# A four-layer image network on one core: in the scans, lines of one pair of images alone at the turns, small products in their pauses, an early pool for the scans' weights, and layer 3's loads in written order

## The chip, the cores and the metric

The kernel runs on one core of one Trainium2 chip. The metric is the device time of one execution in microseconds (us). Three runs of the kernel before gave a median of 13183.47 us (13182.98 to 13188.03).

The core has five engines that matter here, each with an instruction order of its own: TensorE (PE, matrix products), VectorE (DVE), ScalarE (ACT), GpSimd (POOL) and SyncE (SP, which only starts transfers). ACT and POOL can start transfers too. A profile row "L678 PE" is what line 678 of the kernel gave to PE.

## The reference, cut to what matters

The input is four images of 48 channels, 256 by 256, in fp32. Four layers each add something to the image. Layers 1 and 2 are the scans that the change is mostly about:

```python
def step(w, b):
    def f(carry, inp):
        nxt = inp + _conv1d(carry, w, b)     # 5 taps, 48 -> 48 channels, along the line
        return (nxt, nxt)
    return f
...
_, d_rest = jax.lax.scan(step(down_w, down_b), d0, xs[1:])    # rows, from above
...
_, u_rest = jax.lax.scan(step(down_w, down_b), u0, seq)       # rows, from below
...
_, r_rest = jax.lax.scan(step(right_w, right_b), r0, ws[1:])  # columns
...
_, l_rest = jax.lax.scan(step(left_w, left_b), l0, R[Ww - 2::-1])
...
x = x + _L0_conv_ref(_gn(x), ...)   # 1x1, depthwise 3x3, gate, 1x1, filter on 8x8 patches
x = x + _L1_conv_ref(_gn(x), ...)   # the four scans
x = x + _L2_conv_ref(_gn(x), ...)   # the four scans, other weights
x = x + _L3_conv_ref(_gn(x), ...)   # 1x1, filter on 8x8 patches, depthwise 3x3, gate, 1x1
```

`_gn` is a group normalization over the whole image, so each layer needs the statistics of all of its input. In a scan each line of the image (a row or a column) needs the line before it: 256 lines in each of four directions, two layers, and no line of one image can be computed beside another of the same image.

## The kernel before

**Stages.** `input_stats` loads the input and takes its statistics. `layer0` runs with an order that a planner has written out for PE, DVE and ACT. `scans` does layers 1 and 2, `layer3` the last one. They follow one another; the scans run from about 3021 to 8550 us.

**The scans.** The four images are two pairs, A (p=0) and B (p=1). A line of a pair holds 96 partitions: the two interleaved halves of the line times 48 channels, and 256 columns for the two images. One line is three fp32 products into one PSUM tile (`conv`, L678; the profile records each as two rows, six rows a line) and one DVE instruction that adds bias and input and writes the line (the evict): L766 in the down pass, L804 up, L843 right, L881 left. The next line of the same pair reads that line, so a pair alternates between PE and DVE. Two pairs are therefore interleaved: while DVE evicts A's line, PE has B's.

**The order of the two.** `pair(p)` is a Python generator which yields after each line and between the pieces of a normalization (`norm_steps`). `scans` calls the two in turn, one step each a round, and B begins when `count` is 10. The order in which the instructions are written in this loop is the order on PE and on DVE (both are under `manual_schedule`), and it is fixed: if A's instruction waits, B's behind it on the same engine waits too. The other engines' instructions are placed by the scheduler. 36 small products (`WARM`, L704) stand in front of the first line.

**The turns.** Each pass of `scan_layer` goes in blocks of eight lines (`RB`). Down loads the input (L741 and, for the first block, 16 small loads at L750, on SP), scales it on ACT (L757, L761) and stores its lines to `dn`. Up reads `dn` (from its second block on), and ACT copies its lines to `blk` (L811), which goes to `up` (L816). Right reads `up` transposed (L831, on SP). Its first lines need the last rows of the up pass, through the copy, the store and the load; L840 copies its first line from that load. Left takes the lines of right from SBUF and then from `rt`, adds them onto a block of the input (L891; on POOL, and on DVE for the last block of the pass) and stores the sum (L897). It also takes the statistics of the new image (`bn_stats`, made as small functions in `fresh` and written at L904). Then `norm_steps` turns these into scale and shift: L109 aggregates, then two small products (L112, L120) with DVE and ACT pieces between them (L114 to L132).

**Weights.** `scan_weights` makes one direction's weight tile from ten small transfers and two for the bias (L648, L651). Layer 1's down weights are loaded when the scans open (on ACT's queue); right and left follow after A's first down pass, on SP's. Layer 2's are loaded between B's passes. A queue takes its transfers in order: what an issue waits for, all later ones on that engine wait for.

**Layer 0's and layer 3's start.** Both load weights on SP: layer 0 at L191 to L215, then scale and shift (`scp`, L240) and the raw image (L250); ACT normalizes it (L259), and the first product is at L289. Layer 3 fetches a raw strip (L956), copies the scale (`scp`, L945), loads `wi` (L965) and `mk_in` (L966), an identity (L979), depthwise and output weights (L984 to L1005), normalizes on ACT (L1024) and transposes on PE (L1039). Of the engines it fixes PE, DVE and ACT; SP is left to the scheduler.

Of the kernel before, what the change touches and what calls it, by code (L numbers as in the profile page):

```python
# [17 lines left out]
C = 48  # L18
# [11 lines left out]
WARM = 36  # L30


class Net:
# [63 lines left out]
    def norm_steps(self, stats, grp, name="", psum=None):  # L97

        nc, n, rows = self.nc, len(stats), stats[0].shape[0]
        with ExitStack() as st:  # L100
# [7 lines left out]
            for p in range(n):  # L108
                nc.vector.bn_aggr(mv[:, p, :], stats[p])  # L109
                yield  # L110
            pm = psum("pm")
            nc.tensor.matmul(pm, grp, mv[:, :, 0], start=True, stop=True)  # L112
            yield
# [4 lines left out]
            yield  # L118
            pv = psum("pv")
            nc.tensor.matmul(pv, grp, col(2), start=True, stop=True)  # L120
            yield
            nc.vector.tensor_scalar(col(3), pv, EPS, None, ALU.add)  # L122
            nc.scalar.activation(col(4), col(3), AF.Sqrt)  # L123
            yield
# [511 lines left out]
    def scan_weights(self, n, which, eng=None):  # L636


        nc, eng = self.nc, eng or self.nc.sync
        w = self.wp1.tile([CC, 3, CC], F32, name=f"w{n}_{which}", tag=f"w_{which}")  # L640
        b = self.wp1.tile([CC, 1], F32, name=f"b{n}_{which}", tag=f"b_{which}")
        nc.gpsimd.memset(w, 0.0)
        taps = self.a[f"L{n}_{which}_w"]
        for e in range(2):
            for f in range(2):
                lo, hi = (1 if e < f else 0), (2 if e > f else 3)
                for t in range(lo, hi):
                    eng.dma_start(  # L648
                        w[e * C : (e + 1) * C, t, f * C : (f + 1) * C], taps[:, 2 * t + e - f, :]
                    )  # L650
            eng.dma_start(b[e * C : (e + 1) * C, :], self.a[f"L{n}_{which}_b"])  # L651
        self.scan_w[n, which] = w, b

    def open_scans(self, st):
# [6 lines left out]
        self.lines, self.turn, self.scan_w = [], [0] * self.NP, {}  # L661
        self.scan_weights(1, "down", self.nc.scalar)
# [18 lines left out]
    def scans(self, first, stats):  # L681
# [18 lines left out]
        with self.tc.manual_schedule(engines={mybir.EngineType.PE, mybir.EngineType.DVE}):  # L700
            with self.tc.tile_pool(name="ps_w", bufs=1, space=PSUM) as psw:
                warm = psw.tile([128, 128], F32, name="warm")
                for _ in range(WARM):
                    self.nc.tensor.matmul(warm, self.ident, self.ident, start=True, stop=True)  # L704
            going, count = [pair(p) for p in range(self.NP)], 0
            while going:
                for p, g in enumerate(list(going)):
                    if count >= (2 * RB - 6) * p and next(g, g) is g:
                        going.remove(g)
                count += 1  # L710
        return last

    def scan_layer(self, n, p, x, xout, scs, stats):
# [20 lines left out]
        for h0 in range(0, H, RB):  # L734
# [3 lines left out]
            for f in range(2):  # L738
# [8 lines left out]
                for lo, hi in ((1, WB), (0, 1)):  # L747
                    for i in range(2):
                        for e in range(2):
                            nc.sync.dma_start(  # L750
                                half(t, f)[:, i, e, lo:hi].rearrange("p v h w -> p v (h w)"),
                                rows[:, i, e, lo:hi].rearrange("c v h w -> c v (h w)"),
                            )
            for i in range(2):
# [24 lines left out]
        if n == 1 and p == 0:  # L779
            self.scan_weights(1, "right")  # L780
            self.scan_weights(1, "left")
# [41 lines left out]
        for w0 in range(0, W, RB):  # L823
# [3 lines left out]
            for lo, hi in ((1, HB), (0, 1)) if w0 < 2 * RB else ((0, HB),):  # L827
                for e in range(2):
                    for i in ((0, 1), (1, 2)) if w0 < 2 * RB else ((0, 2),):
# [6 lines left out]
                        )  # L836
            for r in range(RB):
# [20 lines left out]
        for w0 in range(W - RB, -1, -RB):  # L858
# [29 lines left out]
            for lo, hi in ((0, RB), (RB, M)) if w0 == 0 else ((0, M),):  # L888
                for f in range(2):
# [3 lines left out]
                    )  # L893
                for e in range(2) if k == 0 else ():
# [10 lines left out]
        for f in fresh:  # L905
            f()

    def layer3(self, x, scs):  # L910
# [11 lines left out]
        with ExitStack() as st:  # L922
# [4 lines left out]
            st.enter_context(tc.manual_schedule(engines=FIXED))  # L927
# [35 lines left out]
            for lo, at, n in parts:  # L963
                for b in range(2):
                    nc.sync.dma_start(wi[64 * b : 64 * b + C, at : at + n], self.a["L3_w_in"][:, lo : lo + n])  # L965
                nc.sync.dma_start(mk_in[:, at : at + n], self.a["L3_fft_mask"][:, lo : lo + n])  # L966
# [448 lines left out]
def net_kernel(ctx: ExitStack, tc: tile.TileContext, args, out, shape):  # L1415
# [4 lines left out]
    first = net.layer0(scs, stats)  # L1420
    with ExitStack() as st:
        net.open_scans(st)
# [100 lines left out]
```

## Time and profile before

| what | value |
|---|---|
| median of three runs | 13183.47 us |
| profiled execution | 13184.79 us |
| span of that execution, first to last instruction | 13182.9 us |
| PE busy | 12347.8 us (94%) |
| DVE busy | 7413.1 us (56%) |
| ACT busy | 3603.9 us (27%) |
| mean granted clock of TensorE | 0.969 |
| first product of layer 0 | at 245.6 us |
| first conv of the scans | at 3040.4 us |
| last evict of the scans | at 8549.7 us |
| layer 3's first normalization (L1024) | at 8580.8 us |

Times of instructions are us from the start of the span. A row of the groups or of the timeline gives the duration, engine, line, output and inputs; in brackets is how long the engine was idle before the instruction and what ended that idle time. A row of the stretches gives for each engine its busy time and, in brackets, its instructions, then the clock that TensorE was granted as a fraction of full speed, then how busy the DMA engines were and what they moved. Busy time of PE is modelled from pipelined products.

### The profile page before, as it was taken

What the parts mean: (1) busy time and instruction counts of PE and PEld (TensorE: products, weight loads), DVE (VectorE), ACT (ScalarE), POOL (GpSimd) and SP (SyncE); (2) the same over time, 40 slices, a digit from 0 to 9 for tenths busy, and PEclk for the clock granted to TensorE, in tenths of its full rate; (3) what the DMA queues carried; (4) which work ended last, traced back from release to release, by engine and by line L of the source; (5) the groups of instructions that cost most, each with busy time, mean ns of one, the idle gap of its engine ahead of it and who ended that gap; (6) DMA issues with size and microseconds to landing.
All of it is one profiled execution on the core that took longest, in us unless ns stands there. A gap on an engine that the chain in (4) does not pass through costs nothing.

```text
span 13182.9 us, 432539 instructions
## 1 busy us (share of the span) xinstructions
PE 12347.8 (94%) x203416; PEld 8136.5 (62%) x203416; DVE 7413.1 (56%) x10790; ACT 3603.9 (27%) x4047; POOL 1333.8 (10%) x977
## 2 busy tenths in 40 slices
PE   2999999999999899999998999899999999999999
PEld 1333333336777677767776777666666666666666
DVE  6777777773333334653333346566666666666666
ACT  1444444442223100012232000033333333333333
POOL 0111010100000002530000015400000000000000
PEclk9999999998999999999999999899999999999999
DMA  7222222226755876987657769711111111111110
GB/s 174 57 57 58 57 55 58 59 48 114 152 141 152 168 153 152 229 174 152 135 151 169 153 134 225 183 25 28 28 23 28 24 26 28 23 27 23 27 28 21
DMA packets 1170373, 1225.00 MB, mean 93 GB/s; under 512 B 1027668, under 2 KB 1031756, under 8 KB 1107724
## 3 DMA queue, kind: packets, MB, share of 16 engines
q1 hardware_dynamic: 1067660, 624.28, 25.0%
q0 software_dynamic: 87488, 445.55, 11.8%
q10 hardware_dynamic: 13440, 127.50, 5.2%
q8 instruction: 1592, 26.08, 0.9%
q14 instruction: 193, 1.58, 0.0%
HBM read 699.76 MB, written 497.42 MB: 91 GB/s over the span
## 4 chain that ended last, share of the span: by engine, by line
PE 88%; ACT 4%; DVE 3%; issue 3%; DMA 2%; SPq 0%; ACTq 0%; POOL 0%; DVEq 0%
PE acc L678 41%; PE pd L1156 13%; PE pd L312 9%; PE pd L1172 5%; PE pz L1073 4%; PE pp L1120 4%; PE po L1248 2%; PE ph L289 2%; PE pz L1086 2%; PE ph L281 1%; PE py L386 1%; DMA gx<-in_x 1%; PE po L456 1%; PE py L393 1%; PE po L1238 1%
## 5 line engine op out<-in xcount | busy, mean ns | idle before, releaser
L678 PE MATMUL acc<-line,w_down 96*96 96x256 f32 x12240 | 2693.4, 382 | 36.3 <-DVE line L766 17.8
L678 PEld LDWEIGHTS acc<-line,w_down 96*96 96x96 f32 x12240 | 2007.8, 164 | 713.4 <-DVE line L766 32.5
L1156 PE MATMUL pd<-z_a,diag 32*32 32x512 f32 x37152 | 1628.5, 598 | 78.9 <-issue 71.2
L312 PE MATMUL pd<-main,diag 32*32 32x512 f32 x36864 | 1419.3, 619 | 55.0 <-issue 52.1
L678 PE MATMUL acc<-line,w_right 96*96 96x256 f32 x6120 | 1338.1, 379 | 82.0 <-issue 39.8
L678 PE MATMUL acc<-line,w_left 96*96 96x256 f32 x6120 | 1360.6, 384 | 27.3 <-DVE line L881 27.3
L1216 DVE SCALAR_TENSOR_TENSOR acc<-z_b,wd,acc 128x1024 f32<-128x1024 f32 (+1 forms) x1056 | 1325.8, 1258 | 34.2 <-ACT acc L1211 6.9
L349 DVE SCALAR_TENSOR_TENSOR acc<-rest,wd,acc 128x1024 f32<-128x1024 f32 x1024 | 1256.4, 1284 | 127.9 <-ACT acc L343 104.8
L1156 PEld LDWEIGHTS pd<-z_a,diag 32*32 32x32 f32 x37152 | 879.1, 103 | 636.9 <-issue 270.9
L678 PEld LDWEIGHTS acc<-line,w_right 96*96 96x96 f32 x6120 | 998.8, 163 | 411.5 <-DVE line L840 40.7
L678 PEld LDWEIGHTS acc<-line,w_left 96*96 96x96 f32 x6120 | 1007.0, 165 | 371.6 <-DVE line L881 41.5
L312 PEld LDWEIGHTS pd<-main,diag 32*32 32x32 f32 x36864 | 502.8, 105 | 767.1 <-issue 650.5
L1172 PE MATMUL pd<-z_b,diag 32*32 32x512 f32 x18432 | 966.6, 636 | 0.7 <-ACT z_b L1032 0.7
L766 DVE TENSOR_TENSOR line<-acc,in 96x256 f32<-96x256 f32 x1020 | 429.1, 421 | 949.5 <-PE acc L678 939.4
L843 DVE SCALAR_TENSOR_TENSOR line<-acc,b_right,in 96x256 f32<-96x256 f32 x1020 | 489.4, 480 | 835.5 <-PE acc L678 835.5
L804 DVE SCALAR_TENSOR_TENSOR line<-acc,b_down,in 96x256 f32<-96x256 f32 x992 | 476.0, 480 | 810.5 <-PE acc L678 810.5
L881 DVE SCALAR_TENSOR_TENSOR line<-acc,b_left,in 96x256 f32<-96x256 f32 x992 | 475.9, 480 | 557.4 <-PE acc L678 557.3
L123 ACT ACTIVATE nrm<-nrm 96x2 f32<-96x2 f32 (+1 forms) x7 | 1.4, 203 | 2823.4 <-DVE nrm L122 2783.6
L891 POOL TENSOR_TENSOR blk<-blk,line 96x1024 f32<-96x1024 f32 x248 | 705.8, 2876 | 638.0 <-DVE line L881 638.0
L811 ACT COPY blk<-line 96x1024 f32<-96x1024 f32 (+2 forms) x264 | 480.1, 1891 | 989.9 <-DVE line L804 803.9
L1076 DVE TENSOR_TENSOR z<-pz,mask 128x1024 f32<-128x1024 f32 x512 | 599.3, 1218 | 265.5 <-PE pz L1073 262.6
L1120 PEld LDWEIGHTS pp<-c_inv,z 64*64 64x64 f32 x32768 | 515.5, 135 | 225.3 <-issue 199.6
(169 smaller groups left out, 13063.5 us busy)
## 6 DMA issues: line engine op xcount, KB each, us to landing
blk<-x ACTq DMA_DIRECT2D x64, 1536.0 KB, 17.8
in<-x SPq DMA_DIRECT2D x248, 384.0 KB, 11.0
dn<-line POOLq DMA_DIRECT2D x124, 768.0 KB, 9.4
rt<-line POOLq DMA_DIRECT2D x124, 768.0 KB, 9.7
in<-rt SPq DMA_DIRECT2D x124, 768.0 KB, 10.8
in<-dn SPq DMA_DIRECT2D x120, 768.0 KB, 5.3
in<-up SPq DMA_DIRECT2D x240, 384.0 KB, 10.8
up<-blk POOLq DMA_DIRECT2D x56, 1536.0 KB, 15.1
```

Of the source, the lines that this page charges most:

```text
L312: nc.tensor.matmul(pd[32 * j : 32 * j + 32, i], diag[s, t, :], z[s, R2 * j + t // 3 : R2 * j + t // 3 + R2, t % 3 : t % 3 + W], start=(t = ...
L349: nc.vector.scalar_tensor_tensor(to, at(t, r), wd[:, 1, t : t + 1], to, ALU.mult, ALU.add)
L678: self.nc.tensor.matmul(acc, w[:, t, :], carry[:, :, t : t + m], start=(t == 0), stop=(t == 2))
L811: nc.scalar.copy(blk[:, :, e, lo:hi, k // 2 : k // 2 + RH], inner(ln[:, e::2])[..., lo:hi].rearrange("p h i w -> p i w h"),)
L843: nc.vector.scalar_tensor_tensor(blocks(inner(line)), blocks(acc), br, new, ALU.add, ALU.add)
L891: (nc.vector if w0 == 0 else nc.gpsimd).tensor_tensor(part, part, inner(ln[:, f::2])[..., lo:hi].rearrange("p w i h -> p i h w"), ALU.add)
L1073: nc.tensor.matmul(pz[:, b, q, :], xf[s, q0 + q, :], wi[s, NM * k : NM * k + NM], start=True, stop=True)
L1076: nc.vector.tensor_tensor(zs[k][:, q0 : q0 + 4].rearrange("p q b c -> p b q c"), pz, mask[:, :, :, NM * k : NM * k + NM].to_broadcast([128 ...
L1120: nc.tensor.matmul(pp[64 * c : 64 * c + 64, l, q, :], z[f, q0 + q, b, 64 * c : 64 * c + 64], self.inv1[f, :], start=True, stop=True,)
L1156: nc.tensor.matmul(pd[32 * j : 32 * j + 32, i, 0:n, :], diag[s, 2 if g == "m" else half, t, :], zt[g][s, R2 * j + t // 3 : R2 * j + t // 3 ...
L1172: nc.tensor.matmul(pd[to, i], diag[s, half, t, :], zt[f"b{half}"][s, R2 * j + t // 3 : R2 * j + t // 3 + R2, t % 3 : t % 3 + W], start=(t ...
L1216: nc.vector.scalar_tensor_tensor(acc, at(t), wd[:, half, t : t + 1], acc, ALU.mult, ALU.add)
```

## The change

There are four parts.

First, the scans' order. `pair` may yield a number instead of nothing. When it does and both pairs are active, two small products are written, and then the other pair does that many steps alone, each followed by two small products. The numbers are 2 before layer 2's first activations, 10 before a first right line, and 0 (two products, no lines) after each DVE piece of a normalization, each of the four additions of the last left block and each two of the last four statistics. When only one pair is active, each round ends with two small products. B begins at 11 rounds instead of 10. A yield of any kind takes a step of its own, and the other pair goes on with a line in it; so at a turn the other pair does 12 lines in a row, at a layer's end some 16. The small products write a PSUM tile that stays open through the scans; those in front are 60 instead of 36.

Second, the scans' weights live in a pool of their own which is opened before layer 0, and all three tiles of layer 1 are loaded there, on SP's queue, before layer 0's weights (36 transfers).

Third, half of the first block's loads of A in layer 1 go on ACT's queue.

Fourth, in layer 3 SP's order is as written, and the twelve loads of `wi` and `mk_in` go on ACT's queue.

```diff
-WARM = 36
+WARM = 60
+LEAD = 16
...
             for p in range(n):
                 nc.vector.bn_aggr(mv[:, p, :], stats[p])
-                yield
+                yield 0
...
-        w = self.wp1.tile([CC, 3, CC], F32, name=f"w{n}_{which}", tag=f"w_{which}")
-        b = self.wp1.tile([CC, 1], F32, name=f"b{n}_{which}", tag=f"b_{which}")
+        w = self.sw.tile([CC, 3, CC], F32, name=f"w{n}_{which}", tag=f"w_{which}")
+        b = self.sw.tile([CC, 1], F32, name=f"b{n}_{which}", tag=f"b_{which}")
...
-        self.lines, self.turn, self.scan_w = [], [0] * self.NP, {}
-        self.scan_weights(1, "down", self.nc.scalar)
+        self.warm = pool("ps1_w", 1, space=PSUM).tile([128, 128], F32, name="warm")
+        self.lines, self.turn = [], [0] * self.NP
...
-            going, count = [pair(p) for p in range(self.NP)], 0
+            def warm(k):
+                for _ in range(k):
+                    self.nc.tensor.matmul(self.warm, self.ident, self.ident, start=True, stop=True)
+
+            going, count = {p: pair(p) for p in range(self.NP)}, 0
+
+            def line(p):
+
+                got = next(going[p], going)
+                if got is going:
+                    del going[p]
+                return got
+
+            warm(WARM)
             while going:
-                for p, g in enumerate(list(going)):
-                    if count >= (2 * RB - 6) * p and next(g, g) is g:
-                        going.remove(g)
+                active = [p for p in range(self.NP) if p in going and count >= (LEAD - 5) * p]
+                for p in active:
+                    alone = line(p) if p in going else None
+                    if isinstance(alone, int) and len(active) > 1:
+                        warm(2)
+                        for _ in range(alone):
+                            for other in [o for o in going if o != p]:
+                                line(other)
+                                warm(2)
+                if len(going) < 2 or count < LEAD:
+                    warm(2)
                 count += 1
...
-                            nc.sync.dma_start(
+                            (nc.scalar if f and n == 1 and p == 0 else nc.sync).dma_start(
...
+            if h0 == 0 and n == 2:
+                yield LEAD - 14
...
-        if n == 1 and p == 0:
-            self.scan_weights(1, "right")
-            self.scan_weights(1, "left")
...
+            if w0 == 0:
+                yield LEAD - 6
...
+                    if w0 == 0:
+                        yield 0
...
-        for f in fresh:
+        for k, f in enumerate(fresh):
             f()
+            if k % 2:
+                yield 0
...
-            st.enter_context(tc.manual_schedule(engines=FIXED))
+            st.enter_context(tc.manual_schedule(engines=FIXED | {mybir.EngineType.SP}))
...
-                    nc.sync.dma_start(wi[64 * b : 64 * b + C, at : at + n], self.a["L3_w_in"][:, lo : lo + n])
-                nc.sync.dma_start(mk_in[:, at : at + n], self.a["L3_fft_mask"][:, lo : lo + n])
+                    nc.scalar.dma_start(wi[64 * b : 64 * b + C, at : at + n], self.a["L3_w_in"][:, lo : lo + n])
+                nc.scalar.dma_start(mk_in[:, at : at + n], self.a["L3_fft_mask"][:, lo : lo + n])
...
-    first = net.layer0(scs, stats)
     with ExitStack() as st:
+        net.sw, net.scan_w = st.enter_context(tc.tile_pool(name="w1s", bufs=1)), {}
+        for which in ("down", "right", "left"):
+            net.scan_weights(1, which)
+        first = net.layer0(scs, stats)
         net.open_scans(st)
```

In `norm_steps` all six bare `yield`s become `yield 0`.

More of the change, by code (lines that the diff above doesn't have):

```diff
@@ L109, in norm_steps @@
                 nc.vector.bn_aggr(mv[:, p, :], stats[p])
-                yield
+                yield 0
             pm = psum("pm")
             nc.tensor.matmul(pm, grp, mv[:, :, 0], start=True, stop=True)
-            yield
+            yield 0
             nc.vector.tensor_copy(col(0), pm)
@@ L117, in norm_steps @@
             nc.vector.tensor_tensor(col(2), col(2), mv[:, :, 1], ALU.add)
-            yield
+            yield 0
             pv = psum("pv")
             nc.tensor.matmul(pv, grp, col(2), start=True, stop=True)
-            yield
+            yield 0
             nc.vector.tensor_scalar(col(3), pv, EPS, None, ALU.add)
             nc.scalar.activation(col(4), col(3), AF.Sqrt)
-            yield
+            yield 0
             nc.vector.reciprocal(col(5), col(4))
@@ L700, in scans @@
         with self.tc.manual_schedule(engines={mybir.EngineType.PE, mybir.EngineType.DVE}):
[L701 to L704, printed above, removed]
-            going, count = [pair(p) for p in range(self.NP)], 0
-            while going:
-                for p, g in enumerate(list(going)):
-                    if count >= (2 * RB - 6) * p and next(g, g) is g:
-                        going.remove(g)
+            def warm(k):
[8 more added lines that the diff above has]
+            warm(WARM)
+            while going:
+                active = [p for p in range(self.NP) if p in going and count >= (LEAD - 5) * p]
[9 more added lines that the diff above has]
+                    warm(2)
                 count += 1
@@ L893, in scan_layer @@
                     )
+                    if w0 == 0:
+                        yield 0
                 for e in range(2) if k == 0 else ():
@@ L904, in scan_layer @@
                     fresh.append(lambda to=to, t=t: nc.vector.bn_stats(to, t))
-        for f in fresh:
+        for k, f in enumerate(fresh):
             f()
+            if k % 2:
+                yield 0
     def layer3(self, x, scs):
```

## The prediction

> **What bounds the kernel now.** I read the page first: busy shares, slices, the chain that ended last.
>
> ```profile
> span 13182.9 us, 432539 instructions
> ...
> PE 12347.8 (94%) x203416; PEld 8136.5 (62%) x203416; DVE 7413.1 (56%) x10790; ACT 3603.9 (27%) x4047; POOL 1333.8 (10%) x977
> ...
> PEclk9999999998999999999999999899999999999999
> ...
> PE 88%; ACT 4%; DVE 3%; issue 3%; DMA 2%; SPq 0%; ACTq 0%; POOL 0%; DVEq 0%
> ```
>
> TensorE is 94% busy, and the change adds products to it, so only the places where it waits or runs slowly can give time. The scans run from 3021.3 to 8550 us. They do 4080 lines (12,240 + 6,120 + 6,120 rows of L678 at six rows a line). Next I asked for stretches (columns: stretch, length, PE busy, PEld, DVE, ACT, POOL, granted clock, DMA share, GB/s):
>
> ```profile
> 3020.00:3101.00 81.00, 56.79 (x173) 35.13 (x174) 15.30 (x42) 9.55 (x12) 5.28 (x19) 0.58 0.58 92
> 3200.00:3450.00 250.00, 250.00 (x1160) 188.53 (x1159) 81.22 (x193) 56.75 (x49) 23.48 (x24) 1.00 0.75 152
> 4380.00:4412.00 32.00, 11.44 (x51) 8.09 (x50) 4.52 (x10) 7.63 (x6) 1.10 (x2) 0.73 0.86 201
> 4450.00:4475.00 25.00, 4.58 (x16) 2.81 (x15) 1.46 (x4) 3.94 (x4) 2.31 (x4) 0.62 0.97 225
> 5750.00:5792.00 42.00, 31.65 (x96) 20.19 (x95) 25.09 (x50) 6.44 (x8) 12.38 (x8) 0.67 0.66 132
> 5811.00:5841.00 30.00, 20.59 (x50) 12.50 (x51) 15.05 (x32) 3.08 (x5) 3.18 (x5) 0.56 0.78 166
> 8493.00:8550.00 57.00, 42.09 (x94) 23.30 (x94) 22.99 (x45) 0.20 (x1) 8.61 (x7) 0.54 0.22 55
> ```
>
> The second row is the steady state: 250 us for 1160 rows, so 0.2155 us a row and 1.293 us a line. 4080 lines need 5276 us of the 5529 that they take. Some 252 us are lost, nearly all in the other rows. The timeline shows how, first at a turn, then at the end:
>
> ```profile
> 4389.33 0.48 DVE L804 SCALAR_TENSOR_TENSOR line<-acc,b_down,in 96x256 f32<-96x256 f32 x1 [0.87 <-PE acc L678]
> 4389.87 1.54 PE L678 MATMUL acc<-line,w_down 96*96 96x256 f32 x6 [0.63 <-DVE line L804]
> 4410.95 0.29 DVE L840 COPY line<-in 96x256 f32<-96x256 f32 x1 [21.13 <-DMA in<-up]
> 4411.34 1.99 PE L678 MATMUL acc<-line,w_right 96*96 96x256 f32 x4 [19.93 <-issue]
> ```
>
> ```profile
> 8515.80 2.87 PE L678 MATMUL acc<-line,w_left 96*96 96x256 f32 x6 [0.57 <-DVE line L881]
> 8519.25 2.87 PE L678 MATMUL acc<-line,w_left 96*96 96x256 f32 x6 [0.57 <-DVE line L881]
> ```
>
> At a turn DVE's fixed order puts A's first right line next. It waits 21.1 us for what the up pass has only just stored, and B's ready line stands behind it. At the end one pair is alone at half clock: 3.45 us a line.
>
> **The change, part by part.** *A line alone.* It is conv, then evict, then conv: at full clock 1.54 + 0.03 + 0.54 (evict start to next conv) = 2.11 us, or 2.05 where the evict is L766 (0.42 for 0.48). Against 1.293 in company it loses 0.82 (0.76). The pause in PE is about 0.8 us. Two small products are four rows; L704's take 0.111 us each at full clock, so 0.44 us, which the pause hides. Without that cover they cost 0.44 a line. On this row the rule of the Trainium skill bears ("TensorE: Matmul & The Clock Gate", Part 1 and "HAM oscillation"): the clock halves after an idle window of some 3.4 us, returns after a busy one[...]. Rows first: between 8510 and 8550 no gap exceeds 0.6 us and modelled PE is 0.83 busy, yet the clock stays at 0.50. So short gaps do keep it low. By the rule the small products would be ballast, and each stretch would pay 2.11 a line from its second window on; by the row a stretch that once fell pays 3.45, the products being what lifts it (1.54 + 0.44 of 2.11 is 0.94 busy). I go by the row; the sum for stretches that enter at full clock is the same by both.
>
> *Turns (four).* Lost now: 4389.87 to 4411.34 is 21.5 us, less 1.3 for the line in it, plus some 2.5 at the low clock after it: 22.7 each. In the new order 12 lines of the other pair stand there, 12 × 2.11 = 25.3 us, over a load that needs 21 to 22 from the last evict. Loss 12 × 0.82 = 9.8. Gain 12.9 × 4 = 52. Bounds 40 (loads 3 us late everywhere) to 55. What is late next is that load, with 3 us to spare.
>
> *Layer boundaries (two).* In 5757.5–5791.4 DVE does four L891 additions (4.35 us), L904 and two L109 (1.86 each) while B's evict stands behind; lost against the steady rate are 21.8 us here and 20.3 in 5811–5841. After: some 16 lines alone between these pieces, 16 × 0.79 = 12.6, plus 2 for an L109 that exceeds a pause: 14.6. Gain 7.2 + 5.7 = 13; bounds 5 to 15 (loads held up behind the weights' issues).
>
> *End.* 15 lines at 3.45 from 8493.2 to 8549.7 lose 37.1. After, DVE's work lies between lines and the clock holds: 15 × 0.82 + 2 = 14.5. Gain 22.6; bounds 20 to 23.
>
> *Start.* The first conv is at 3040.4 now (behind w_down, landing late after ten issues on ACT's queue); 16 lines at 3.39 follow, and B starts at 3100.7. Lost: 64.9. After: the weights are there and half of the loads go on ACT's queue; 60 products with 2 more are 26 more than 36, 52 rows × 0.111 = 5.8 us past 3031.2, so 3037. Then 16 × 2.05 + 0.7 (four products in some rounds) + 2.0 (L109) = 35.5, and B's first line waits some 7.5 us for its norm (statistics to scale to line, two transfers: 8.9 us now). Clock lost there again. Loss 43.9; gain 21, bounds 15 to 24.
>
> *Layer 3's start.* The same queue and these rows:
>
> ```profile
> 8556.29 2.92 SPq L966 DMA_DIRECT2D mk_in<-in_L_fft_mask  x1
> 8559.26 5.72 SPq L965 DMA_DIRECT2D wi<-in_L_w_in  x2
> 8573.08 2.94 SPq L945 DMA_DIRECT2D scp<-sc  x2
> 8580.80 4.04 ACT L1024 ACTIVATE u<-raw,scp 112x256 f32<-112x256 f32 x8 [18.00 <-DMA scp<-sc]
> ```
>
> The scale is ready at 8563.9 but its copy stands behind 12 weight loads on SP until 8573.1. After, these are on ACT's queue, which holds u itself: ten before the square root L123, two after. Gain 9; bounds 3 (ACT's issues take the 2.9 us seen here) to 14. SP in written order elsewhere: a raw fetch in layer 3 is issued 39 us and more before use; nothing there waits.
>
> *Weights early: the part that costs.* 36 small loads now stand ahead of layer 0's own on SP, whose first waits for the same end of the statistics:
>
> ```profile
> 221.25 0.31 SPq L191 DMA_DIRECT2D wi<-in_L_w_in  x1
> 232.87 2.48 SPq L240 DMA_DIRECT2D scp<-sc  x4
> 235.39 10.93 SPq L250 DMA_DIRECT2D raw<-in_x  x6
> 243.20 2.31 ACT L259 ACTIVATE xn<-raw,scp 112x2304 f32<-112x2304 f32 x1 [12.12 <-DMA raw<-in_x]
> ```
>
> From 221.25 to 232.87 24 loads issue, 0.484 each, and the chain goes through them: then scp, raw, xn, first product at 245.6. 36 × 0.484 = 17.4 later. Low end 15; high 23 (0.64, as w_down's slower issues on ACT's queue). Nothing hides it, as TensorE has no other work then. The other loads of weights were hidden (right and left at 3685–3698 beside full PE).[...] The row (0.484) decides.
>
> Sum: 52 + 13 + 22.6 + 21 + 9 − 17.4 = 100.2. The span becomes 13082.7; the execution shown was 1.9 above its span at 13184.8, and the median of the runs shown is 13183.5, 0.6 above the span. So 13083. With every bound at its worse end the gain is 40 + 5 + 20 + 15 + 3 − 23 = 60 (13123), at its better 114 (13069).
>
> **Rivals.** *Loads still late at turns and boundaries.* The up pass stores and A's loads share the DMA with B's own; DMA is at 0.9 there. If each load comes 5 us beyond its cover, and half clock follows for 3 us, 7 us × 6 = 42 come off: 13125. For it: 3 us to spare; against: the stores and loads are issued as before.
>
> *The clock isn't held (the other side).* If lines alone run at 3.45 at every turn and boundary, a turn loses 12 × 2.16 + 2 = 28, against 22.7 now (−21 for four); a boundary 16 × 2.16 = 34.5 (−27 for two); the end gains nothing, the start 5. −21 − 27 + 5 + 9 − 17 = −51: 13235. It decides when more than two thirds of these lines run at half clock. Against it: stretches enter from a full PE, and even at half clock the two products (0.85 us) fill the 0.8 us pause, which lifts it again.
>
> *The queue of early weights is slow.* Where a load here takes 2.9 us, as beside stores at 8556, 36 cost 104 and the gain is 117.6 − 104 = 13: no change, 13170. Against it: at 221 no other traffic runs.
>
> **How the numbers follow.** The sum as worked out 0.70; late loads 0.17; slow queue 0.06; half clock 0.05; other 0.02. A measurement here tells 0.2%, 26 us. Faster (below 13157) is the first two and a little, 0.88; same 0.07; slower 0.05. The likeliest is 13083; its own bounds are 13069 to 13123. The range takes late loads in to 13135 and leaves out about 2 in 10, with 13060 below for a cheaper queue than 15.
>
> **What would show it.** Right: no PE gap over 2 us at the turns (4389 and 4450 here); lines alone at 2.1 with clock 1.00; first layer-0 product 17 us later; end lines at 2.1; u 9 us sooner after the last evict. Wrong: clock 0.50 over the new alone stretches; a DVE wait for in<-up of over 3 us; first product in layer 0 past 270.

## The result, and the profile after

The changed kernel took 13145.72 us, the median of nine runs (13126.85 to 13164.83), against 13188.03 us for the kernel before beside it. The ratio is 0.9968, 95% interval [0.9958, 0.9979]: 42 us, or 0.32%, faster. A second comparison of the same two kernels on another chip gave 0.9966 [0.9953, 0.998]. The forecast was 13083 us, 100 us faster, with a range of 13060 to 13135. The sign was right; the gain was forecast at more than twice what came, and the time lies 11 us above the range.

The profiled execution of the changed kernel was the slowest of its nine (13164.83 us, 19 above their median), so its span of 13163.1 us shows only 20 of the 42 us. First the page's spans, busy shares, slices and chain:

```profile
span 13163.1 us, 433663 instructions
...
PE 12389.6 (94%) x203960; PEld 8201.4 (62%) x203960; DVE 7421.7 (56%) x10790; ACT 3604.7 (27%) x4047; POOL 1331.7 (10%) x977
...
PEclk9999999999999999999999999999999999999999
...
PE 88%; ACT 4%; issue 3%; DVE 3%; DMA 2%; SPq 1%; POOL 0%; ACTq 0%; DVEq 0%; POOLq 0%
```

The two slices in which the clock fell below 0.9 (slice 10 and the one at the end of the scans) are gone. SP's queue now has 1% of the chain, where it had none. The stretches that answer to those shown of before (start, steady state, A's turn, B's turn, B's second turn, the two halves of the boundary, the end):

```profile
3060.00:3123.00 63.00, 53.77 (x312) 45.23 (x313) 15.58 (x42) 12.37 (x14) 4.48 (x16) 0.89 0.65 113
3200.00:3450.00 250.00, 250.00 (x1160) 188.45 (x1159) 81.25 (x194) 58.35 (x50) 23.55 (x24) 1.00 0.75 152
4400.00:4430.00 30.00, 27.78 (x138) 20.71 (x137) 7.42 (x17) 11.41 (x8) 1.10 (x2) 1.00 0.80 206
4440.00:4490.00 50.00, 36.95 (x164) 26.79 (x163) 9.79 (x21) 4.06 (x4) 3.46 (x5) 0.83 1.00 204
7150.00:7197.00 47.00, 36.14 (x164) 26.36 (x163) 9.47 (x21) 3.97 (x4) 3.17 (x4) 0.89 0.96 200
5750.00:5800.00 50.00, 44.00 (x212) 32.76 (x211) 35.84 (x64) 5.61 (x7) 14.92 (x9) 0.97 0.49 111
5800.00:5850.00 50.00, 48.18 (x238) 36.11 (x238) 24.03 (x54) 11.23 (x12) 4.54 (x7) 1.00 0.85 156
8471.00:8510.00 39.00, 31.87 (x156) 23.60 (x155) 26.82 (x45) 0.20 (x1) 9.60 (x7) 0.96 0.33 82
```

The steady state is the same to the row. A's turn is closed, at full clock. B's turns still have holes and a low clock (0.83 and 0.89), and the DMA share is 1.00 and 0.96 there: that is the first surprise.

To see where the time went I cut each trace into stages. For the scans, the loss of a stretch is its length less its rows of L678 (L679 after) times 0.2155 us. Where A's turn ends and B's begins is a choice that moves up to 2 us from one to the other. A gain is positive:

| stage | before | after | gain | forecast |
|---|---|---|---|---|
| end of statistics to layer 0's first product | 24.4 | 41.8 | -17.4 | -17.4 |
| layer 0, first product to first small product | 2775.7 | 2793.4 | -17.7 | 0 |
| loss at the scans' start | 64.7 | 41.7 | 23.0 | 21 |
| loss at A's two turns | 23.3 + 23.1 | 9.9 + 11.7 | 24.8 | 26 |
| loss at B's two turns | 22.8 + 23.1 | 25.0 + 20.0 | 0.9 | 26 |
| loss at the boundaries, both halves | 43.6 | 31.2 | 12.4 | 13 |
| loss at the end | 38.1 | 20.3 | 17.8 | 22.6 |
| last evict to layer 3's first u | 30.8 | 28.4 | 2.4 | 9 |
| layer 3 from its first u | 4602.4 | 4625.0 | -22.6 | 0 |

The statistics ended 4.7 us later in the trace of after; that end lies between 219.8 and 235.8 in all traces here, with and without the change, and belongs to the loads of the input. Three things need a cause: B's turns, and layers 0 and 3, whose products the change does not touch.

The queue at layer 0's start, in the timeline of the changed kernel:

```profile
226.28 4.57 SPq L649 DMA_DIRECT2D w_down<-in_L_down_w  x10
...
242.81 0.42 SPq L192 DMA_DIRECT2D wi<-in_L_w_in  x1
...
254.55 2.48 SPq L241 DMA_DIRECT2D scp<-sc  x4
...
265.21 2.31 ACT L260 ACTIVATE xn<-raw,scp 112x2304 f32<-112x2304 f32 x1 [28.65 <-DMA raw<-in_x]
```

The 36 loads start at 225.88 and layer 0's first load issues at 242.81: 16.9 us, 0.470 each. From there on the row is the old one, shifted.

### The profile page after: what moved, and what is told of

Its sections match the earlier page's. It is cut to its first block, busy times and chain, and to the rows that moved or that the text cites. A ratio compares the mean times of both kernels' runs of the same rounds, so it can differ in the third digit from the quotient of the medians.

```text
span 13163.1 us, 433663 instructions
## 1 busy us (share of the span) xinstructions
PE 12389.6 (94%) x203960; PEld 8201.4 (62%) x203960; DVE 7421.7 (56%) x10790; ACT 3604.7 (27%) x4047; POOL 1331.7 (10%) x977
## 4 chain that ended last, share of the span: by engine, by line
PE 88%; ACT 4%; issue 3%; DVE 3%; DMA 2%; SPq 1%; POOL 0%; ACTq 0%; DVEq 0%; POOLq 0%
PE acc L679 40%; PE pd L1179 13%; PE pd L313 9%; PE pd L1195 5%; PE pz L1096 4%; PE pp L1143 4%; PE po L1271 2%; PE ph L290 2%; PE pz L1109 2%; PE ph L282 1%; PE py L387 1%; DMA gx<-in_x 1%; PE po L457 1%; PE py L394 1%; PE po L1261 1%
## 5 line engine op out<-in xcount | busy, mean ns | idle before, releaser
L679 PE MATMUL acc<-line,w_down 96*96 96x256 f32 x12240 | 2661.0, 379 | 14.6 <-ACT line L777 5.0
L679 PEld LDWEIGHTS acc<-line,w_down 96*96 96x96 f32 x12240 | 1989.3, 163 | 671.5 <-DVE line L821 11.5
L679 PE MATMUL acc<-line,w_right 96*96 96x256 f32 x6120 | 1340.2, 380 | 25.1 <-DVE line L859 19.9
L679 PE MATMUL acc<-line,w_left 96*96 96x256 f32 x6120 | 1336.6, 379 | 9.9 <-DVE line L900 7.5
L679 PEld LDWEIGHTS acc<-line,w_right 96*96 96x96 f32 x6120 | 997.3, 163 | 356.2 <-DVE line L859 20.7
L679 PEld LDWEIGHTS acc<-line,w_left 96*96 96x96 f32 x6120 | 994.7, 163 | 338.5 <-DVE line L900 16.4
L124 ACT ACTIVATE nrm<-nrm 96x2 f32<-96x2 f32 (+1 forms) x7 | 1.4, 203 | 2801.7 <-DVE nrm L123 1428.9
```

Of the source, the lines that this page charges most:

```text
L679: self.nc.tensor.matmul(acc, w[:, t, :], carry[:, :, t : t + m], start=(t == 0), stop=(t == 2))
```

## The experiments

All kernels were timed beside the kernel before on the same chip; ratios are to it. Chips differ: the kernel before took 13188, 13232, 13225, 13239 and 13210 us in five sessions. So times of different sessions are compared by their ratios, and stages by their durations. Executions differ too: nine of the kernel before beside each other lay between 13201.5 and 13265.8 us. A stage's duration comes from one execution each, and a difference of 10 or 20 us in a single trace is no result.

### The loads of the early weights, put behind layer 0's own

```diff
     with ExitStack() as st:
         net.sw, net.scan_w = st.enter_context(tc.tile_pool(name="w1s", bufs=1)), {}
+        first = net.layer0(scs, stats)
         for which in ("down", "right", "left"):
             net.scan_weights(1, which)
-        first = net.layer0(scs, stats)
```

> The changed kernel with the three early weight tiles still in their early pool, but their 36 loads written behind layer 0's own (SP issues them some six raw strips later). Theory, the loads on the chain: from the end of the statistics to layer 0's first product 24 us as before instead of 41.8, so about 17 us under the changed kernel, some 59 under the kernel before. Rival, the early pool itself (where tiles lie) makes layer 0 longer: layer 0 stays at 2793 us from first product to first small product, against 2776 before, also here; if that was only chance of this execution it lies anywhere between 2770 and 2795.

Measured: 0.9958 [0.9941, 0.9974]. From the end of the statistics to the first product it is 24.9 us: the 17 us are the queue's, as forecast. By the ratios this kernel is some 12 us under the changed one instead of 17, and the intervals overlap. In its trace layer 0 took 2816.2 us, more than in the changed kernel's (2793.4), so why layer 0 runs longer stayed open.

### Layer 3's loads back on SP

```diff
-            st.enter_context(tc.manual_schedule(engines=FIXED | {mybir.EngineType.SP}))
+            st.enter_context(tc.manual_schedule(engines=FIXED))
...
-                    nc.scalar.dma_start(wi[64 * b : 64 * b + C, at : at + n], self.a["L3_w_in"][:, lo : lo + n])
-                nc.scalar.dma_start(mk_in[:, at : at + n], self.a["L3_fft_mask"][:, lo : lo + n])
+                    nc.sync.dma_start(wi[64 * b : 64 * b + C, at : at + n], self.a["L3_w_in"][:, lo : lo + n])
+                nc.sync.dma_start(mk_in[:, at : at + n], self.a["L3_fft_mask"][:, lo : lo + n])
```

> The changed kernel with its fourth part undone: wi and mk_in on SP again, SP left to the scheduler in layer 3. Theory, the fourth part is worth little: last evict to first u 31 instead of 28.4 us, so 2 to 3 us slower than the changed kernel, and the 22.6 us that layer 3 took longer (4625 against 4602 from the first u) are chance. Rival, SP in written order slows layer 3: it goes back to about 4602, and this kernel is some 20 us faster than the changed one.

Measured: 0.9950 [0.9936, 0.9965]. From the last evict to the first u 31.2 us (28.4 with the part), as the theory has it; layer 3 took 4624.6 us, not 4602. But the theory had this kernel 2 to 3 us slower than the changed one, and by the ratios it is some 22 us faster, as the rival said, though not in the stage that the rival named. The intervals just overlap.

### No products in the pauses

```diff
                     if isinstance(alone, int) and len(active) > 1:
-                        warm(2)
                         for _ in range(alone):
                             for other in [o for o in going if o != p]:
                                 line(other)
-                                warm(2)
-                if len(going) < 2 or count < LEAD:
-                    warm(2)
```

> The changed kernel without the small products in the pauses; the 60 in front stay, the order of the lines too. Theory, short gaps hold a low clock down: wherever the clock has fallen in a stretch of lines alone it stays at 0.50 to the end of the stretch, 3.4 us a line; the start loses about 20 us more (16 lines if it falls at once, fewer if later), the second turn of each layer up to 10 each, the end up to 18: 20 to 60 us slower than the changed kernel. Stretches that are entered at full clock keep 2.11. Rival[...]: within 5 us of the changed kernel.

Measured: 0.9994 [0.9985, 1.0003], some 34 us slower than the changed kernel by the ratios, inside the 20 to 60 forecast; the rival, that the products do not matter (5 us), falls. The scans took 5503.4 us instead of 5448.8: 55 us lost. The same line alone, in this kernel's timeline of PE, first at A's turn, then in the boundary:

```profile
4417.09 1.54 PE L679 MATMUL acc<-line,w_down 96*96 96x256 f32 x6 [0.64 <-DVE line L817]
4419.19 1.54 PE L679 MATMUL acc<-line,w_down 96*96 96x256 f32 x6 [0.57 <-DVE line L817]
...
5831.96 2.87 PE L679 MATMUL acc<-line,w_down 96*96 96x256 f32 x6 [0.51 <-DVE line L782]
5835.35 2.87 PE L679 MATMUL acc<-line,w_down 96*96 96x256 f32 x6 [0.51 <-DVE line L782]
```

and its stretches:

```profile
4400.00:4436.00 36.00, 29.06 (x123) 18.72 (x121) 9.93 (x21) 11.41 (x8) 1.10 (x2) 1.00 0.89 200
5782.00:5880.00 98.00, 84.14 (x186) 46.82 (x185) 38.18 (x80) 15.85 (x18) 10.41 (x10) 0.50 0.53 119
```

With the same gaps of 0.5 to 0.6 us the clock holds at 1.00 where the stretch is entered at full clock, for all 12 lines (25 us), and stays at 0.50 where it fell once: from 5774 for 109 us, from 8521 for 85. In the changed kernel's trace no drop in the scans lasts longer than 17 us. So the products are not needed to hold the clock up at A's turn; they bring it back where it fell.

### The early weights alone, on the kernel before

```diff
-        w = self.wp1.tile([CC, 3, CC], F32, name=f"w{n}_{which}", tag=f"w_{which}")
-        b = self.wp1.tile([CC, 1], F32, name=f"b{n}_{which}", tag=f"b_{which}")
+        w = self.sw.tile([CC, 3, CC], F32, name=f"w{n}_{which}", tag=f"w_{which}")
+        b = self.sw.tile([CC, 1], F32, name=f"b{n}_{which}", tag=f"b_{which}")
...
-        self.scan_weights(1, "down", self.nc.scalar)
...
-    first = net.layer0(scs, stats)
     with ExitStack() as st:
+        net.sw, net.scan_w = st.enter_context(tc.tile_pool(name="w1s", bufs=1)), {}
+        for which in ("down", "right", "left"):
+            net.scan_weights(1, which)
+        first = net.layer0(scs, stats)
```

> The kernel before with the second part alone: early pool, layer 1's three weight tiles loaded on SP before layer 0's. Theory: first product 17 us later, first conv some 3 us sooner after layer 0 (no wait for w_down at 3040.4), nothing else: 14 us slower than the kernel before. Rival, the early pool also makes layer 0 longer by some 18 us: 30 us slower.

Measured: 1.0018 [1.0009, 1.0028], 24 us slower (12 to 37), which takes in both the theory's 14 and the rival's 30. First product 41.6 us after the statistics (+17.2); layer 0 took 2815.7 us (+40 in this trace). In the trace, then, the early weights cost more than their queue.

### Seven and 22 lines alone at B's turns

```diff
-                yield LEAD - 6
+                yield (LEAD - 6, 5)[p]
```

> The changed kernel with 7 lines alone at B's turns instead of 12 (5 in the yield). Theory, A's own loads delay B's: from B's last up evict to its first right line less than the 35 to 37 us of 12 lines and more than the 22 of none, 25 to 33 us, so the stall there is 10 to 18 us. Rival, the load takes 36 us for another reason (the written order of the queue): 36 again, and the stall is 21 us.

> The changed kernel with 22 lines alone at B's turns instead of 12 (20 in the yield). Theory, A's own loads delay B's: 22 lines cover 46 us; the load has landed by then unless it comes later still with each of A's blocks. If it lands at 36 to 42, no stall, and the turn loses 22 x 0.82 = 18 us plus nothing; if A's further blocks hold it up, a stall of some us stays even here.

In the second the number is 20. Each is a single execution, so only its trace is read. The answer is in DVE's timeline at B's first turn: its last evict of the up pass, and the copy of its first right line. First the kernel before, then the changed kernel, then seven lines:

```profile
4449.79 0.48 DVE L804 SCALAR_TENSOR_TENSOR line<-acc,b_down,in 96x256 f32<-96x256 f32 x1 [0.82 <-PE acc L678]
...
4472.65 0.29 DVE L840 COPY line<-in 96x256 f32<-96x256 f32 x1 [21.09 <-DMA in<-up]
```

```profile
4440.35 0.48 DVE L821 SCALAR_TENSOR_TENSOR line<-acc,b_down,in 96x256 f32<-96x256 f32 x1 [0.81 <-PE acc L679]
...
4477.65 0.29 DVE L859 COPY line<-in 96x256 f32<-96x256 f32 x1 [12.28 <-DMA in<-up]
```

```profile
4453.30 0.48 DVE L821 SCALAR_TENSOR_TENSOR line<-acc,b_down,in 96x256 f32<-96x256 f32 x1 [0.81 <-PE acc L679]
...
4486.21 0.29 DVE L859 COPY line<-in 96x256 f32<-96x256 f32 x1 [18.48 <-DMA in<-up]
```

With A standing still the copy starts 22.9 us after the last evict; with seven lines of A in between 32.9; with twelve 37.3 (34.6 to 38.0 in 14 such turns of seven traces). Past twelve it is no later: with 22 lines the load had landed 35.3 us after the last evict. So most of the delay is there as soon as the other pair runs, and past twelve lines it does not grow. The rival, 36 in any case, is not far off: seven lines took off 2 to 5 us, in one turn. At A's turn the other pair is in its up pass and the load comes within its 12 lines in every trace. Most of the time goes on SP's queue. The load is four transfers; first the kernel before, where all four are issued, then the changed kernel, where the first three are:

```profile
4456.80 9.72 SPq L831 DMA_DIRECT2D in<-up  x4
```

```profile
4450.03 22.80 SPq L848 DMA_DIRECT2D in<-up  x3
```

The first of the three stood 16.9 us at its issue, with the DMA share at 1.00. B's own last stores (L833) landed 33.2 us after the last evict instead of 22.2. In the changed kernel a load of the input's next block (`blk<-x`, L888, 1536 KB, on ACT's queue) and two of A's stores of right lines (L866) instead of one fall into this stretch; the kernel before issues no `blk<-x` until B's load is there. Which of A's transfers is in the way was not separated. With 22 lines there is no wait at B's first turn, and that turn loses 18.0 us, as 22 × 0.82 says. But the kernel took 13341.7 us, and the one with seven 13255.4, for the reason that the next one shows.

### A mended version that wasn't one

```diff
-                yield LEAD - 6
+                yield (LEAD - 6, 16)[p]
```

with the weights' loads behind layer 0's and layer 3's loads back on SP, as above.

> The changed kernel with the loads of the early weights behind layer 0's own, layer 3's loads back on SP, and 18 lines alone at B's turns instead of 12. Theory: 17 us from layer 0, about 10 to 15 from B's two turns (18 lines cover 38 us against a load of 35 to 37; 18 x 0.82 = 15 lost instead of 20 to 25), 3 lost at layer 3's start; some 25 us under the changed kernel, 90 under the kernel before. Rival: the longer A runs on alone the later B's load comes (it shares the transfers with A's), so B's turns still end in a stall of 5 us or more, and only the 17 are gained.

Measured: 1.0005 [0.9993, 1.0016]: the whole gain is gone. B's turns came as the theory has it: no wait for the first right line, and some 15 us lost over the 18 lines of each; behind the first turn some 6 more went to a later load. But 18 lines instead of 12 leave the pairs six lines further apart at each of the two turns, and nothing closes the distance again: when B ends its right pass, A is 21 lines into its left pass in layer 1 and 27 in layer 2, where the changed kernel has 15 in both and the kernel before 14. The scans lose 83 us between 7280 and 8400, in layer 2, where the changed kernel loses 3.4. The timeline there:

```profile
8064.99 0.48 DVE L900 SCALAR_TENSOR_TENSOR line<-acc,b_left,in 96x256 f32<-96x256 f32 x1 [0.21 <-PE acc L679]
8089.34 5.64 POOL L910 TENSOR_TENSOR blk<-blk,line 96x1024 f32<-96x1024 f32 x2 [24.80 <-DMA blk<-x]
8092.20 0.69 DVE L925 BATCH_NORM_STATS2 st<-blk 96x6 f32<-96x512 f32 x1 [26.72 <-POOL blk L910]
```

The block of the input comes late, POOL's addition waits 24.8 us for it, DVE's statistics wait 26.7 for POOL, and every evict stands behind them. The other traces show that it is the distance, and in both directions. Left passes entered at 10, 14, 15 and 21 lines lose 1 us or less between their ends; those entered at 25, 27 and 35 lose 42, 86 and 74, and one entered at 5 loses 36 (5, 10, 25 and 35 are from the kernels with seven and 22 lines, one execution each). Layer 1 of this kernel, at 21, lost nothing: 18 lines did no harm there, only their repetition in layer 2. Why the block comes late at such a distance (A and B share three block buffers) was not taken further, and a kernel that closes the six lines again was not run.

### The changed kernel once more, and before twice more

> The changed kernel once more, unedited. The stages that the change touches sum to 65 us less than before in its first trace (start of layer 0 +17, scans -80, start of layer 3 -2). Theory: layers 0 and 3 differ between executions by chance (2776 to 2816 and 4602 to 4640 so far), so with more runs the time comes to some 65 us under the kernel before, and the two layers come out elsewhere in their ranges. Rival: something in the change makes layer 3 about 20 us longer, so the time stays at some 42 under, and layer 3 again takes 4620 or more.

> The kernel before, unedited, for a second look at its layers 0 and 3. Theory, chance of the clock: layer 3, from its first u, which took 4602 and 4604 in the two traces with the old order of the scans and 4625 to 4656 in eight with the new one, lies anywhere between 4600 and 4650; layer 0 between 2775 and 2816. Rival, the new order leaves layer 3 in a worse state: here it is 4602 to 4606 again.

> The kernel before, unedited, for a third look: as for the second.

The changed kernel: 0.9966 [0.9953, 0.998], layer 0 2800.6, layer 3 4638.0. The kernel before: layer 0 2777.8 and 2780.2, layer 3 4623.6 and 4613.5. Layer 3 does vary, by 21 us in three traces of one kernel; layer 0 before hardly varies. The changed kernel came 45 us under the kernel before (26 to 62): the theory's 65 lies just outside, and its layer 3 above 4620, as the rival said. The two single executions of the kernel before took 13210.3 and 13209.0 us.

### Parts one and three, with the weights behind layer 0

The weights' loads behind layer 0's and layer 3's loads back on SP (both edits above), 12 lines at B's turns.

> The changed kernel with the loads of the early weights behind layer 0's own and layer 3's loads back on SP; 12 lines alone at B's turns as in the change. Theory: stages sum to 83 us (scans) under the kernel before, start of layer 0 and of layer 3 as before, so 83 under, 17 to 20 under the changed kernel, if layers 0 and 3 are the same by the mean. Rival, layer 3 is about 25 us longer behind the new order of the scans: 55 to 60 under.

Measured: 0.9946 [0.9929, 0.9962], 71 us faster. Layer 0 2788.3, layer 3 4633.9. It lies between the theory's 83 and the rival's 55 to 60, with both inside its interval (50 to 94 us).

### One part alone, three times

First the kernel before with an idle tile held beside layer 0:

```diff
-    first = net.layer0(scs, stats)
+    with tc.tile_pool(name="gap", bufs=1) as gap:
+        nc = tc.nc
+        nc.gpsimd.memset(gap.tile([CC, 3 * (3 * CC + 8)], F32, name="gap"), 0.0)
+        first = net.layer0(scs, stats)
```

> The kernel before with one idle tile of 3552 bytes a partition held beside layer 0, so that layer 0's tiles lie where the early pool puts them; no loads are moved. Layer 0 took 2776, 2778 and 2780 us in three traces of the kernel before and 2788 to 2816 in ten with the early pool. Theory, placement: layer 0 at 2795 or more, the kernel 15 to 25 us slower than before. Rival, the 36 loads in front do it (or chance): 2775 to 2785, same time as before.

Then the scans' order alone, written here against the changed kernel, with layer 3's edit of above beside it:

```diff
-        w = self.sw.tile([CC, 3, CC], F32, name=f"w{n}_{which}", tag=f"w_{which}")
+        w = self.wp1.tile([CC, 3, CC], F32, name=f"w{n}_{which}", tag=f"w_{which}")
...
+        self.scan_weights(1, "down", self.nc.scalar)
...
-                            (nc.scalar if f and n == 1 and p == 0 else nc.sync).dma_start(
+                            nc.sync.dma_start(
...
+        if n == 1 and p == 0:
+            self.scan_weights(1, "right")
+            self.scan_weights(1, "left")
...
-        for which in ("down", "right", "left"):
-            net.scan_weights(1, which)
```

> The first part alone: new order of the scans with the small products; weights, first loads and layer 3 as before. Theory: layer 0 at 2776 to 2780 as the pool is not early, scans 75 to 80 us shorter; if layer 3 is as in the kernel before (4602 to 4624) the kernel is 75 to 80 us faster, the best so far. Rival, layer 3 is longer behind the new order (4625 to 4656 so far): some 50 to 55.

And the fourth part alone, on the kernel before:

```diff
-            st.enter_context(tc.manual_schedule(engines=FIXED))
+            st.enter_context(tc.manual_schedule(engines=FIXED | {mybir.EngineType.SP}))
...
-                nc.sync.dma_start(mk_in[:, at : at + n], self.a["L3_fft_mask"][:, lo : lo + n])
+                nc.scalar.dma_start(mk_in[:, at : at + n], self.a["L3_fft_mask"][:, lo : lo + n])
```

(the same for `wi`).

> The fourth part alone: wi and mk_in on ACT's queue, SP in written order in layer 3; all else as before. Theory, it gives 2 us at layer 3's start and nothing else: layer 3 from its first u at 4602 to 4624. Rival, SP in written order makes layer 3 longer (six traces with it: 4625 to 4656): 4630 or more, 15 to 25 us slower than before.

The idle tile alone: 1.0004 [0.9993, 1.0015], layer 0 2784.7. The place of the tiles gives at most a small part. The fourth part alone: 1.0005 [0.9993, 1.0017], layer 3 4625.6, from last evict to u 28.6. No gain is seen; what it saves at the start is too small to show in the time.

The order of the scans alone (weights, first loads and layer 3 as before): 0.9940 [0.9925, 0.9954], 79 us faster and nearly twice the gain of the whole change. It is the lowest ratio of all, though its interval overlaps those of 0.9946 and 0.9950 above. Layer 0 takes 2776.8 us again, layer 3 4608.8, so the rival falls: the new order of the scans alone does not lengthen layer 3. Its start shows what the early weights and ACT's loads had bought: the scans' start loses 48.5 us instead of 41.7. Those 7 us are all.

### Idle loads

```diff
+    with tc.tile_pool(name="gap", bufs=1) as gap:
...
+        t = gap.tile([CC, 3 * (3 * CC + 8)], F32, name="gap")
+        nc.gpsimd.memset(t, 0.0)
+        for k in range(40):
+            nc.sync.dma_start(t[0:C, 2 * k : 2 * k + 1], args["L1_down_b"])
+        first = net.layer0(scs, stats)
```

> The kernel before with an idle tile of 3552 bytes a partition beside layer 0 and 40 idle loads of 192 bytes into it, on SP, within layer 0's own. Theory A, any such loads in front lengthen layer 0 itself: 2795 or more (with the tile alone 2785, with the 36 weight loads 2788 to 2816). Theory B, it is the position in the eight lanes that transfers take in turn (36 leaves a remainder of 4, 40 none): here 2785 as with the tile alone, and 2795 or more with 36. First product some 18 us later in any case.

> As with 40 idle loads, but 36. Theory A: layer 0 at 2795 or more in both. Theory B: 2795 or more here alone. If both stay near 2785, the lengthening belongs to neither and stays open.

On the kernel before; a single execution each. First product 43.2 and 41.6 us after the statistics; layer 0 2828.8 us with 40 and 2818.0 with 36. So it is not the turn of the lanes; such loads lengthen layer 0 with 40 as with 36. The stretches of layer 0, with 36 idle loads and then with the tile alone:

```profile
1000.00:2000.00 1000.00, 918.09 (x18263) 371.30 (x18247) 729.71 (x972) 425.28 (x409) 97.63 (x93) 0.95 0.27 57
2000.00:3000.00 1000.00, 926.15 (x18283) 376.51 (x18266) 725.65 (x961) 430.89 (x411) 97.29 (x94) 0.94 0.26 55
```

```profile
1000.00:2000.00 1000.00, 918.84 (x18330) 371.06 (x18315) 732.78 (x976) 437.31 (x422) 102.52 (x94) 0.96 0.26 56
2000.00:3000.00 1000.00, 929.54 (x18833) 379.99 (x18817) 745.01 (x986) 435.11 (x419) 99.56 (x92) 0.97 0.25 55
```

PE is as busy, gets through fewer products, and has a clock of 0.94 to 0.95 instead of 0.96 to 0.97. The loss is not at the start: it grows along the layer. With the weight loads the clock doesn't tell as much: its mean over layer 0 is 0.951 to 0.961 in the ten traces with them and 0.958 to 0.962 in the six without any added loads, and in the longest of the ten (2816.2 us) it is 0.957, while PE is idle for 231 us instead of 205 to 220.

Over all traces: layer 0 took 2775.4 to 2780.2 us in the five without moved loads or tile, and 2788.3 to 2816.2 in the ten with the early weights (mean 2801.7 against 2777.2: 24.5 us), in front of its loads or behind them. With the tile alone it took 2784.7, so all twelve traces with added loads lie above all six without. That loads added at layer 0's start lengthen it is shown. How they do so for the rest of the layer, with the same orders on PE, DVE and ACT, stays open. Layer 3 took 4602 to 4636 in eleven traces without the fourth part and 4625 to 4656 in seven with it. The two overlap, and another line divides them better: the nine traces that have the early weights and the new order together lie at 4625 to 4656, with the part or without it, and the eight that have at most one of the two, and not the part, at 4602 to 4624. The part alone lies between, at 4625.6 in one trace. So the changed kernel's layer 3 is longer than before in every trace, and what does it isn't settled.

## Why the prediction was wrong

- *A line alone: right.* 2.11 us (4417.09 to 4419.19 above) and 2.05 at the start. The two small products fit in the pause.
- *The clock's row against the rule: right, for the reason given.* The rule of the Trainium skill ("TensorE: Matmul & The Clock Gate", Part 1) has the clock fall after an idle window of some 3.4 us and return after a busy one. The first half fits A's turns without the products, where gaps of 0.57 us left the clock at 1.00. For the second half, the prediction read the rule as if modelled 0.83 busy were a busy window; it wasn't enough: with gaps of 0.5 to 0.6 us a fallen clock stayed at 0.50 for 109 us, and without the products 55 us of the scans' gain were lost. The prediction said where: a stretch that once fell.
- *A's turns: right.* Losses 9.9 and 11.7, forecast 9.8.
- *B's turns: the first step that failed, worth 26 us.* "In the new order 12 lines of the other pair stand there, 12 × 2.11 = 25.3 us, over a load that needs 21 to 22 from the last evict." The 21 to 22 came from a trace in which the other pair stood still. With its lines running the load took 35 to 38. In the trace shown stalls of 12.3 and 10.1 us remained, and a clock at half for 17 and 10 us came with them. The four turns gave 25.7 us instead of 52, below the bounds of 40 to 55. The rival of late loads had the mechanism, and named the sign for it (DMA at 0.9 there), but gave it 0.17 and 7 us a place at all six places; it was some 10 to 15 us at two, and none at A's.
- *Boundaries and start: right* (12.4 for 13, 23.0 for 21; of the start's 43.9 the terms written out make only some 38, and the clock's share had no size of its own). *End: mis-sized*, 17.8 for 22.6 and below its bounds of 20 to 23: DVE's pieces still left PE gaps of 1.7 and 2.0 us, and the clock fell at 8496 for 3 us.
- *Layer 3's start: just under its lower bound of 3*, 2.4 for 9. The prediction named it: ACT's issues taking the 2.9 us seen on SP. They took 3.6, and the square root L124, behind ten of them, came 20.0 us after the last evict instead of 12.9:

```profile
8519.82 3.62 ACTq L989 DMA_DIRECT2D mk_in<-in_L_fft_mask  x1
...
8523.48 3.72 ACTq L988 DMA_DIRECT2D wi<-in_L_w_in  x2
...
8529.74 0.20 ACT L124 ACTIVATE nrm<-nrm 96x2 f32<-96x2 f32 x1 [29.75 <-DMA mk_in<-in_L_fft_mask]
```

  I took the value in the middle although the row that it was nearest to, these same loads at the same moment, was at hand.
- *Weights early: right for the queue* (17.4), *and the second step that failed, layer 0*, which the sum held constant. It ran 24.5 us longer by the means of all traces (19 in the two of the changed kernel). "Nothing hides it" was said of the 17; that layer 0 itself would run slower was in no case. The runs show that the added loads do it, and not how.
- *Layer 3 behind its start: held constant too.* It took 4625 and 4638 us in the two traces of the changed kernel and 4602 to 4624 in three of the kernel before, 18 more by the means; the cause is open.

The sum with what was measured: scans 80 (78.9 in the rows), layer 3's start 2.4, queue -17.4 make 65. Less 19 for layer 0 and 18 for layer 3 it is 28, and the measurements are 42 and 45. Without layer 3's share it would be 46. Executions of one kernel differ by more than this, so the sum doesn't tell how much of layer 3's share is in the medians.

## What to carry to other kernels

A load's duration read while its neighbour stands still is not its duration once the neighbour is given work in that gap: where the cover itself uses the same transfers, ask what the load takes beside it. When several edits come together, time each alone before keeping them all: here one of four gave 79 us and the other three together took nearly half of it back. Filling a wait with a different number of lines at each of two turns changes the distance between two interleaved streams; the change adds up from turn to turn, and stages downstream may work only within a range of it (here 10 to 21 lines were good, 5 and 25 were not).

## What the runs showed of the hardware

The clock has a memory: with gaps of 0.57 us after each 1.54 us of products it stays at 1.00 for 25 us when it was there, and with 2.87 us of products and gaps of 0.51 to 0.57 it stays at 0.50 for 109 us when it had fallen. With two small products in each pause (0.44 us at full clock) no drop in the scans lasted longer than 17 us. And 36 or 40 small loads of 192 bytes, or 36 weight loads, at the start of a 2.8 ms stage go with a longer stage: by 11 to 39 us with the weight loads and by 41 and 52 with the small ones, against 2777.2 us (33 and 44 against the kernel with the tile alone). The clock's mean over the stage was 0.947 with the small loads and 0.951 to 0.961 with the weights, where it was 0.958 to 0.962 without.
